# Flamingo block on one core: the last mixture of experts sorted once for all tokens, its tiles run in six steps, with another order of stages

## The chip, the cores and the metric

The kernel runs on one core of a Trainium2 chip. The metric is the device time of one execution in microseconds (us); lower is better. A core has five engines that run at the same time: TensorE (PE; its weight loads are shown as PEld), VectorE (DVE), ScalarE (ACT), GpSimd (POOL) and SyncE (SP), which here only issues DMAs. Each engine takes its instructions strictly in order: an instruction that waits holds all that stand behind it. Sixteen DMA engines move data for all queues. POOL issues the DMAs whose row numbers come from a table (indirect ones); SP issues nearly all others.

## The reference

The input `x` has 16 batches of 256 tokens of 128 values, all float32: 4096 tokens. Four layers follow; each adds a cross attention to a context of 64 keys (16 heads of 8) and then a feed-forward part, both after a layernorm and both times a tanh gate:

```python
x = x + tanh(g_xattn[0]) * L0_xattn(layernorm(x), ctx, ctx, ...)   # softmax over heads
x = x + tanh(g_ffn[0])   * L0_ffn(layernorm(x), ...)               # 8 experts, top 2, and a shared one
x = x + tanh(g_xattn[1]) * L1_xattn(...)                           # with a bias on the scores
x = x + tanh(g_ffn[1])   * L1_ffn(...)                             # ternary weights, 128x128
x = x + tanh(g_xattn[2]) * L2_xattn(...)
x = x + tanh(g_ffn[2])   * L2_ffn(...)                             # comes down to one expert
x = x + tanh(g_xattn[3]) * L3_xattn(...)
x = x + tanh(g_ffn[3])   * L3_ffn(...)                             # 8 experts, top 1: the last mixture
```

The last mixture, which the change is about:

```python
logits = t @ switch_w + switch_b                 # t: 4096 x 128
route_prob = softmax(logits)
route_prob_max, routes = max(route_prob), argmax(route_prob)
for e in range(8):
    h = gelu(t @ w1[e] + b1[e])                  # 128 -> 512
    y = h @ w2[e] + b2[e]                        # 512 -> 128
    out = where(routes == e, y, out)
out = out * route_prob_max
```

## The kernel before

**Halves, stages, blocks.** The 16 batches are cut into two halves of 8. Each half goes through eight stages: 0 and 1 are the first layer's attention and mixture, 2 and 3 the second's attention and ternary product, 4 and 5 the third's attention and expert, 6 and 7 the fourth's attention and mixture. Attention works on a batch, layernorm and feed-forward on a block of two batches (512 tokens, four tiles of 128). `X[i][b]` is the event that batch b has come to stage i. Both halves are under way at once.

**A planner writes the order.** Every piece of work is a generator (a task with a rank) that asks for the next instruction, with an estimated length and the events and buffers that it needs. `Order.run` takes the request that can begin first by these estimates (rounded to 0.1 us), and of several the one with the lowest rank. The result is a fixed order on PE, DVE, ACT, SP and POOL. The plan's times are not waited for on the chip: a DMA task that is planned "when X[5][b] has come" only has its place in SP's order from that. Real waits come from the framework, which follows who writes and reads each tile or tensor. `RANKS` gives each half's eight stages their rank.

**A mixture by sorted tiles.** Tokens are sorted by expert, so that a tile of 128 rows has one expert. For each tile the kernel loads one expert's packed weights (592 KB, `fetch`, L1822, six buffers `wb`), gets the tile's rows, transposes them (L1867), multiplies by W1 (L1881), applies gelu (L1888), multiplies by W2 (L1902), and on DVE adds the bias (L1912) and, in the last mixture, the gate and the old x (L1919). The first mixture gathers rows by an index (L1853, POOL), stores sorted results and collects them (`collect`, L1971 and L1979).

**The last mixture** (`last_mixture`) is run once for each half. A half has a tensor `xrow3{hf}` in HBM with a region of 2048 rows for each of 8 experts, and 128 rows between; a row holds the normed token, the old x, the token's number and its gate (1032 bytes). Each block normalizes, does the gate matmul (L1618), softmax and largest entry, counts how many of its tokens go to each expert (L1653), puts the running counts in `next_`, and POOL scatters its four tiles of rows to their places (L1681). When all four blocks of the half are counted, one table is made on DVE (L1702 to L1739): which expert each tile has, and from which row it starts. Each expert's last tile may be partly empty, so a half has 16 + 7 = 23 tiles, 46 in all. SP fetches a tile's 128 rows at a row number read from the table (L1848). Results are scattered by POOL straight to the output (L1947), empty rows to a number out of bounds.

**Filling.** Since a tile may read rows that no token was put in, `fill_regions` writes defined values into the tensors ahead of time: 27 DMAs of 645 KB for each half (L1804), placed in SP's order by the events X[5] and X[6] of the first half for the first tensor, and X[3] and X[4] of the second half for the second. Other loads on SP at that time are the score bias of the second attention (L312, through three buffers).

Of the kernel before, what the change touches and what calls it, by code (L numbers as in the profile page):

```python
# [75 lines left out]
REGION = NT * P  # L76
NROWS = E * REGION + (E - 1) * P


def sorted_tiles(k):  # L80

    return k * NT + E - 1
# [10 lines left out]
RANKS = ((10, 14, 14, 1, 1, 12, 8, 14), (14, 14, 2, 7, 5, 9, 10, 15))  # L93
# [116 lines left out]
def op(engine, length, *needs, table=None):  # L210
    return ("op", engine, length, needs, table)
# [6 lines left out]
def get(slots, number, *needs):  # L218
    return ("get", slots, number, needs, None)
# [24 lines left out]
def flamingo_kernel(  # L244
# [37 lines left out]
    def slots(name, shape, n, dtype=F32):  # L282
        return Slots([cst(shape, f"{name}_{i}", dtype) for i in range(n)])
# [52 lines left out]
    for l, k in ((0, 2), (3, 1)):  # L336
        n = sorted_tiles(k)
        for hf in range(2):
            size = [NT * P, D] if l == 0 else [NROWS, ROW3]
            xd = dram.tile(size, F32, name=f"xrow{l}{hf}", tag=f"xrow{l}{hf}")  # L340
            yd = None
            if l == 0:
                yd = dram.tile([n * P, D], F32, name=f"ysort{l}{hf}", tag=f"ysort{l}{hf}")
            srt[l, hf] = (k, n, xd, yd)
# [101 lines left out]
    state_s = slots("state", [P, 4 * NT + nmax], 2)  # L446
# [3 lines left out]
    expert_s = slots("expert", [1, 2 * (nmax + 7)], 2, I32)  # L450
# [1126 lines left out]
    def last_mixture(hf, rank, begin):  # L1577
# [6 lines left out]
        _, n, xd, _ = srt[l, hf]  # L1584
        b0 = HB * hf
        blks = range(NBLK // 2 * hf, NBLK // 2 * (hf + 1))
        (st,) = yield get(state_s, 1, begin[b0], moe_ready)
        (ex,) = yield get(expert_s, 1)
        pos = st.ap[:, 0:NT].bitcast(I32)

        next_ = st.ap[:, 4 * NT : 4 * NT + E]
        yield op(DVE, 0.1, st)
        nc.vector.tensor_copy(next_, region)
        kept = Event(len(blks) * 4)
        counted = Event(len(blks))
# [7 lines left out]
        def block(blk):  # L1603
            t0 = 4 * (blk - blks[0])
# [65 lines left out]
            order.set(counted, at)  # L1670
# [7 lines left out]
            for t in range(t0, t0 + 4):  # L1678
                at = yield op(POOL, 1.3, placed)
                part_indirect()  # L1680
                ins = nc.gpsimd.indirect_dma_start(  # L1681
                    out=xd,
                    out_offset=bass.IndirectOffsetOnAxis(ap=pos[:, t : t + 1], axis=0),
                    in_=rows[:, t - t0, :],
                    in_offset=None,
                )
                unordered(ins, f"x{l}{hf}")
                at = (at[0] + 2.2, "DMA")
                order.set(kept, at)
            give(xn, big_s, at)  # L1690

        for blk in blks:
            order.task(rank, block(blk))

        (sc,) = yield get(xf_s, 1, counted)
# [3 lines left out]
        yield op(DVE, 0.6, counted, sc)  # L1701
        nc.vector.tensor_tensor(cn, next_, region, ALU.subtract)  # L1702
        nc.vector.tensor_scalar(cn.bitcast(I32), cn, float(P - 1), None, ALU.add)
        nc.vector.tensor_scalar(cn.bitcast(I32), cn.bitcast(I32), -P, None, ALU.bitwise_and)
        nc.vector.tensor_copy(pad, cn.bitcast(I32))
        nc.vector.tensor_tensor_scan(ends, ones[:, 0:E], pad, 0.0, ALU.mult, ALU.add)
        nc.vector.tensor_scalar(skip, pad, -1.0, float(REGION), ALU.mult, ALU.add)
# [19 lines left out]
        known = yield op(DVE, 0.0026 * n * (E - 1) * 2 + 0.15)  # L1727
        by_tile(skip[:, 0 : E - 1], sums)
        nc.vector.tensor_tensor(rowf, sums, starts[:, 0:n], ALU.add)
        nc.vector.tensor_copy(ex_r, rowf[0:1])  # L1730

        filled, empty = (st.ap[:, NT + n * i : NT + n * (i + 1)].bitcast(I32) for i in range(2))
        at = yield op(DVE, 1.1)
        nc.vector.tensor_tensor(skip[:, 0 : E - 1], next_[:, 1:], next_[:, 0 : E - 1], ALU.subtract)
        by_tile(skip[:, 0 : E - 1], sums)
        nc.vector.tensor_scalar(sums, sums, next_[:, 0:1], None, ALU.add)
        nc.vector.scalar_tensor_tensor(rowf, rowf, place_of, sums, ALU.add, ALU.is_lt)
        nc.vector.tensor_scalar(filled, rowf, -1.0, None, ALU.mult)
        nc.vector.tensor_scalar(empty, rowf, -2.0 * B * S, 2.0 * B * S, ALU.mult, ALU.add)  # L1739
# [3 lines left out]
        ex.users, st.users = 2 * n, n  # L1743
        order.task(rank, fetch(l, hf, ex, known, room, fetched))
        for q in range((n + 1) // 2):
            order.task(
                rank + 0.001 * q,
                sorted_pair(
                    l, hf, q, st, ex, (at, kept), room[q], fetched[q], None, filled, empty
                ),  # L1750
            )
# [33 lines left out]
    def unordered(ins, group):  # L1785

        tc.declare_no_dep(ins.ins, group=group, reason="rows are unique")
        tc.add_to_no_dep_group(group, ins.ins)
        scatters.add(ins.ins.name)
# [9 lines left out]
    def fill_regions(hf, whens):  # L1799
        xd = srt[3, hf][2].rearrange("(p a) c -> p a c", p=P)  # L1800
        n, m = NROWS // P, 5
        for i in range(n // m):
            yield dma(SP, 4.0 * P * m * ROW3, whens[i * m * len(whens) // n])
            nc.sync.dma_start(  # L1804
                xd[:, m * i : m * (i + 1), :],
                rows_sb[:, 0:ROW3].unsqueeze(1).to_broadcast([P, m, ROW3]),
            )

# [18 lines left out]
    def sorted_pair(l, hf, q, st, ex, needs, room, fetched, stored, filled=None, empty=None):  # L1827
# [82 lines left out]
        for i in range(m):  # L1910
            yt = yield op(DVE, 0.25 if l == 0 else 0.75, at, y)
            nc.vector.tensor_tensor(  # L1912
                yi[i], py.ap[:, i * D : (i + 1) * D], wb[i].ap[:, PK_B2 : PK_B2 + D],
                ALU.add,
            )
            give(wb[i], wb_s, yt)
            if l == 3:
                t = 2 * q + i
                nc.vector.scalar_tensor_tensor(  # L1919
                    yi[i], yi[i], xg[i][:, 2 * D + 1 :], xg[i][:, D : 2 * D], ALU.mult, ALU.add  # L1920
                )

                nc.vector.tensor_tensor(
                    place[:, i : i + 1], xg[i][:, 2 * D : 2 * D + 1].bitcast(I32),
                    filled[:, t : t + 1], ALU.bitwise_and,
                )
                nc.vector.tensor_tensor(  # L1927
                    place[:, i : i + 1], place[:, i : i + 1], empty[:, t : t + 1], ALU.bitwise_or
                )
                give(xgs[i], xg_s, yt)  # L1930
# [58 lines left out]
    def rank(stage, hf, i=0):  # L1989
        return RANKS[hf][stage] + 0.01 * i  # L1990
# [5 lines left out]
    for hf in range(2):  # L1996
# [26 lines left out]
        order.task(rank(7, hf), last_mixture(hf, rank(7, hf), X[7]))  # L2023

    whens = [X[i][b] for i, h in ((5, 0), (6, 0), (3, 1), (4, 1)) for b in range(HB * h, HB * h + HB)]
    for hf in range(2):
        order.task(100.0, fill_regions(hf, whens[16 * hf : 16 * hf + 16]))
# [92 lines left out]
```

## Time and profile before

Nine runs: median 1078.47 us, 1071.66 to 1086.42. The profiled execution took 1091.43 us, of which the span from the first instruction to the last is 1089.7.

| | busy us | share of the span | in 700 to 900 us |
|---|---|---|---|
| PE | 916.1 | 84% | 191 of 200 |
| PEld | 729.0 | 67% | 134 of 200 |
| DVE | 690.7 | 63% | 150 of 200 |
| POOL | 633.3 | 58% | 114 of 200 |
| ACT | 586.3 | 54% | 130 of 200 |

DMA queues moved 150 MB. Marks on the time line, from the starts of instructions: the first mixture's tiles run from 188 to 317 (first half) and 363 to 530 (second half); the second attention from 388 to 720; the third and fourth from 550 to 950; gate matmuls of the last mixture's eight blocks begin at 812, 857, 875, 897, 918, 939, 953 and 977; its tiles run from 934 to 1080.

A line of instructions in the profile gives the kernel's line, engine, operation, tiles (output, arrow, inputs), count, then busy us and mean ns, then idle time before it and what ended it. "busy" says nothing of whether an instruction's work was on the path to the end; the chain of waits follows that path back from the last instruction.

### The profile page before, as it was taken

How to read it: one execution, taken by the hardware profiler on the slowest of the kernel's cores; microseconds unless marked ns; L12 is line 12 of the kernel's file. 1: busy time of each engine (PE TensorE's matmuls, PEld its weight loads, DVE VectorE, ACT ScalarE, POOL GpSimd, SP SyncE). 2: the span in 40 equal slices, each digit the busy share in tenths (PEclk: the TensorE clock that was granted, in tenths of full speed). 3: DMA queues.
4: the chain of work that ended last, by engine and by line, in shares of the span. 5: the costliest groups of instructions: out<-in, count | busy, mean ns of one | idle time of the engine just before them, and what ended most of it. 6: DMA issues, size and time to landing. Idle time of an engine off the chain costs nothing.

```text
span 1089.7 us, 28097 instructions
## 1 busy us (share of the span) xinstructions
PE 916.1 (84%) x10472; PEld 729.0 (67%) x10472; DVE 690.7 (63%) x2027; ACT 586.3 (54%) x1369; POOL 633.3 (58%) x1032
## 2 busy tenths in 40 slices
PE   5888577979879797889888799999999997977875
PEld 3776345868776686767756577766666664767775
DVE  4797897754348244545667578977766787555333
ACT  6454343675544354666647447675775664654432
POOL 5786636668646746663357554353456786465443
PEclk9898779989989988899989889999999998998988
DMA  6000104366852555564562931999900005277782
GB/s 195 2 12 12 32 1 145 114 229 227 271 144 66 182 165 179 186 215 132 132 123 59 210 77 43 225 223 224 208 6 21 12 26 186 95 248 240 257 291 96
DMA packets 96280, 150.14 MB, mean 138 GB/s; under 512 B 11281, under 2 KB 75800, under 8 KB 96144
## 3 DMA queue, kind: packets, MB, share of 16 engines
q1 hardware_dynamic: 88160, 131.77, 43.6%
q0 software_dynamic: 7552, 15.65, 5.0%
q8 instruction: 82, 1.34, 0.5%
q10 hardware_dynamic: 432, 0.93, 0.3%
q14 instruction: 54, 0.44, 0.1%
HBM read 99.11 MB, written 50.12 MB: 137 GB/s over the span
## 4 chain that ended last, share of the span: by engine, by line
PE 35%; DVE 17%; DMA 6%; POOL 5%; issue 5%; ACT 2%; SPq 1%; POOLq 0%; another core or an unknown queue 0%; DVEq 0%; ACTq 0%
PE bank L1881 6%; PE bank L1902 5%; PE bank L1033 4%; PE bank L1200 3%; DVE mx L1118 3%; DMA xg<-xrow,state 3%; PE bank L1159 2%; PE bank L1097 2%; DMA yg<-ysort,state 2%; PE bank L1039 2%; DVE mx L1071 1%; PE bank L806 1%; PE bank L1222 1%; DVE ln L669 1%; DVE pT L1079 1%
## 5 line engine op out<-in xcount | busy, mean ns | idle before, releaser
L1888 ACT ACTIVATE big<-bank,wb 128x128 f32<-128x128 f32 x496 | 138.7, 380 | 120.3 <-issue 66.2
L1881 PE MATMUL bank<-xgT,wb 128*128 128x128 f32 x992 | 145.2, 300 | 29.4 <-DVE y L1927 15.3
L1881 PEld LDWEIGHTS bank<-xgT,wb 128*128 128x128 f32 x992 | 132.0, 210 | 40.2 <-DVE y L1927 16.9
L1902 PE MATMUL bank<-wb,big 128*128 128x128 f32 x992 | 135.0, 290 | 2.2 <-ACT big L1888 2.0
L1902 PEld LDWEIGHTS bank<-wb,big 128*128 128x128 f32 x992 | 127.9, 205 | 4.9 <-ACT big L1888 2.9
L681 ACT ACTIVATE xn<-x,ln 128x128 f32<-128x128 f32 x224 | 94.1, 493 | 50.9 <-POOL ln L675 50.5
L1971 POOL DMA_INDIRECT yg<-ysort,state x64 | 63.7, 995 | 65.4 <-DMA ysort<-y 29.2
L919 POOL TENSOR_TENSOR pT<-pT,rc 128x1024 f32<-128x1024 f32 x32 | 75.1, 2363 | 37.8 <-DVE rc L902 9.5
L1118 DVE TENSOR_REDUCE mx<-bank 128x8 f32<-128x512 f32 x128 | 81.1, 681 | 15.8 <-PE bank L1039 7.9
L1912 DVE TENSOR_TENSOR y<-bank,wb 128x128 f32<-128x128 f32 x124 | 32.3, 286 | 92.2 <-PE bank L1902 72.8
L1853 POOL DMA_INDIRECT xg<-xrow,state x78 | 76.7, 983 | 13.7 <-issue 7.6
L1033 PE MATMUL bank<-kexp,qT 32*128 32x256 f32 x768 | 74.0, 427 | 11.2 <-DVE pT L1079 10.9
L1947 POOL DMA_INDIRECT out_dram<-y x46 | 46.6, 1012 | 62.8 <-DVE y L1912 57.1
L702 POOL TENSOR_TENSOR x<-x,rows_sb 128x256 f32<-128x256 f32 x96 | 71.8, 764 | 15.5 <-ACT xn L681 14.7
L672 POOL TENSOR_SCALAR ln<-ln 128x4 f32<-128x4 f32 x64 | 14.8, 232 | 110.7 <-DVE ln L670 101.5
L1187 ACT ACTIVATE pT<-bank 128x512 f32<-128x512 f32 x128 | 67.2, 601 | 21.5 <-PE bank L1174 20.6
L1871 DVE COPY xgT<-bank 128x256 f32<-128x256 f32 x64 | 26.3, 413 | 69.4 <-PE bank L1867 52.8
L669 DVE BATCH_NORM_STATS2 ln<-x 128x6 f32<-128x128 f32 x256 | 68.5, 267 | 2.6 <-DMA x<-in_x_dram 2.3
L673 POOL TENSOR_TENSOR ln<-ln,mhalf 128x4 f32<-128x4 f32 x64 | 66.9, 1045 | 5.3
L1103 ACT ACTIVATE pT<-bank 128x512 f32<-128x512 f32 x64 | 37.6, 599 | 39.2 <-PE bank L1097 36.8
L1200 PE MATMUL bank<-pT,vx 128*32 128x256 f32 x768 | 58.3, 401 | 0.2 <-ACT pT L1103 0.2
L1033 PEld LDWEIGHTS bank<-kexp,qT 32*128 32x128 f32 x768 | 37.5, 193 | 23.6 <-DVE pT L1079 12.1
(269 smaller groups left out, 2187.3 us busy)
## 6 DMA issues: line engine op xcount, KB each, us to landing
wb<-in_pk_l_dram SPq DMA_DIRECT2D x124, 578.0 KB
xrow<-rows_sb SPq DMA_DIRECT2D x54, 645.0 KB
xg<-xrow SPq DMA_DIRECT2D x46, 129.0 KB
ysort<-y SPq DMA_DIRECT2D x38, 128.0 KB
fill<-in_fsideT_dram SPq DMA_DIRECT2D x64, 64.0 KB
x<-in_x_dram SPq DMA_DIRECT2D x16, 128.0 KB
xrow<-xn SPq DMA_DIRECT2D x8, 256.0 KB
xg<-xrow,state POOLq DMA_INDIRECT x78
```

The lines of the kernel that those rows point to most:

```text
L669: nc.vector.bn_stats(st[:, 2 * i + j, :], xs[b][:, j, :])
L681: nc.scalar.activation(xn[:, k, :], xs[b][:, j, :], AF.Identity, bias=nm[:, k : k + 1], scale=rs[:, k : k + 1],)
L702: nc.gpsimd.tensor_tensor(xs[b], xs[b], row.unsqueeze(1).to_broadcast([P, 2, D]), ALU.add)
L919: nc.gpsimd.tensor_tensor(s3, s3, rc.ap.unsqueeze(1).to_broadcast([P, 8, P]), ALU.mult)
L1033: nc.tensor.matmul(dst(g), qT[strip(g), ts], kexp[strip(g)].rearrange("p h k -> p (h k)"), start=True, stop=False,)
L1118: nc.vector.tensor_reduce(mx[:, :, g, :], sc[g].ap.rearrange("p (t h k) -> p t h k", h=4, k=S2), AX.X, ALU.max,)
L1187: nc.scalar.activation(pTs[g // 2].ap[:, (g % 2) * 512 : (g % 2 + 1) * 512], sc[g].ap, AF.Exp)
L1200: nc.tensor.matmul(po.ap[strip(g), i * S : (i + 1) * S], vx.ap[:, b % 2, c, :], pTs[c // 4].ap[:, (c % 4) * S : (c % 4 + 1) * S], start=Tr ...
L1853: nc.gpsimd.indirect_dma_start(out=xg[i], out_offset=None, in_=xd, in_offset=bass.IndirectOffsetOnAxis(ap=index[:, 2 * q + i : 2 * q + i + ...
L1881: nc.tensor.matmul(ph.ap[:, cs], wb[i].ap[:, cs], xgT.ap[:, i * P : (i + 1) * P], start=True, stop=True,)
L1888: nc.scalar.activation(two(hb)[:, i, cs], ph.ap[:, cs], func, bias=wb[i].ap[:, PK_B1 + c : PK_B1 + c + 1],)
L1902: nc.tensor.matmul(py.ap[:, i * D : (i + 1) * D], two(hb)[:, i, c * P : (c + 1) * P], wb[i].ap[:, PK_W2 + c * D : PK_W2 + (c + 1) * D], st ...
```

## The change

The last mixture is no longer run for each half. There is one tensor of rows for all 4096 tokens, with regions of 4096 rows, and one running count. Blocks of both halves are put into it as they come. After 3, 4, 5, 6, 7 and 8 blocks a step begins, with 5, 4, 4, 4, 4 and 18 tiles: 39 in all, 32 + 7. So many full tiles there must be after that many blocks, however the tokens fall; tiles of a step but the last are full, so their output needs no marking of empty rows. `held` keeps how much of each region earlier steps have taken. Each step makes a table of its own, and its order is `told` by the step before. A scatter of rows needs, in the plan, that all filling is done; the filling has 53 DMAs of 645 KB, all placed by X[5] of the first half. Ranks of several stages change. The steps' tiles have the rank of stage 7 of the first half (for the first two) or the second.

```diff
-REGION = NT * P
-NROWS = E * REGION + (E - 1) * P
+REGION = B * S
+NROWS = E * REGION + (E + 1) * P
+STEPS = ((3, 5), (4, 4), (5, 4), (6, 4), (7, 4), (8, 18))
...
-RANKS = ((10, 14, 14, 1, 1, 12, 8, 14), (14, 14, 2, 7, 5, 9, 10, 15))
+RANKS = ((8, 14, 14, 11, 1, 11, 11, 16), (14, 14, 2, 14, 5, 12, 13, 15))
+FILL = (5,)
...
-        for hf in range(2):
-            size = [NT * P, D] if l == 0 else [NROWS, ROW3]
-            xd = dram.tile(size, F32, name=f"xrow{l}{hf}", tag=f"xrow{l}{hf}")
...
+    regions = dram.tile([NROWS, ROW3], F32, name="xrow3", tag="xrow3")
+    for i, (_, n) in enumerate(STEPS):
+        srt[3, i] = (1, n, regions, None)
...
-            order.set(counted, at)
+            blocks_counted[0] += 1
+            mine_of = [i for i, (k, _) in enumerate(STEPS) if blocks_counted[0] <= k]
+            for i in mine_of:
+                if blocks_counted[0] == STEPS[i][0]:
+                    nc.vector.tensor_copy(snap[i], upto3[:, :, 4])
+                    order.set(counted[i], at)
...
-                at = yield op(POOL, 1.3, placed)
+                at = yield op(POOL, 1.3, placed, regions_filled)
...
-                unordered(ins, f"x{l}{hf}")
+                unordered(ins, "x3")
                 at = (at[0] + 2.2, "DMA")
-                order.set(kept, at)
+                for i in mine_of:
+                    order.set(kept[i], at)
...
+        for blk in range(NBLK):
+            rank = rank_of(7, blk // (NBLK // 2))
+            order.task(rank, block(blk, rank))
+        ex_at = [sum(n for _, n in STEPS[:i]) for i in range(len(STEPS) + 1)]
+        for i, (k, n) in enumerate(STEPS):
+            order.task(
+                rank_of(7, int(k > NBLK // 2)) + 0.0005 * i,
+                step(
+                    i, n, st, snap[i], held, Slot(ex.ap[:, 2 * ex_at[i] : 2 * ex_at[i + 1]]),
+                    counted[i], kept[i], tables, rank_of(7, int(k > NBLK // 2)) + 0.1 * i,
+                ),
+            )
...
+    def step(i, n, st, seen, held, ex, counted, kept, tables, rank):
+        l, last = 3, i == len(STEPS) - 1
+        (sc,) = yield get(xf_s, 1, counted, tables[i])
...
+        nc.vector.tensor_tensor(cn, seen, region, ALU.subtract)
+        nc.vector.tensor_scalar(cn.bitcast(I32), cn, float(P - 1 if last else 0), None, ALU.add)
...
+        nc.vector.tensor_scalar(skip, pad, -1.0, float(REGION), ALU.mult, ALU.add)
+        nc.vector.tensor_tensor(pad, pad, held, ALU.subtract)
         nc.vector.tensor_tensor_scan(ends, ones[:, 0:E], pad, 0.0, ALU.mult, ALU.add)
+        nc.vector.tensor_tensor(
+            skip[:, 0 : E - 1], skip[:, 0 : E - 1], held[:, 1:], ALU.add
+        )
...
+        else:
+            at = yield op(DVE, 0.3)
+            nc.vector.tensor_tensor(ends, pad, ends, ALU.subtract)
+            nc.vector.tensor_scalar(ends, ends, float(P * n), 0.0, ALU.add, ALU.max)
+            nc.vector.tensor_tensor(ends, ends, pad, ALU.min)
+            nc.vector.tensor_tensor(held, held, ends, ALU.add)
+        order.set(tables[i + 1], at)
...
-    def fill_regions(hf, whens):
-        xd = srt[3, hf][2].rearrange("(p a) c -> p a c", p=P)
+    def fill_regions(whens):
+        xd = regions.rearrange("(p a) c -> p a c", p=P)
         n, m = NROWS // P, 5
         for i in range(n // m):
-            yield dma(SP, 4.0 * P * m * ROW3, whens[i * m * len(whens) // n])
+            at = yield dma(SP, 4.0 * P * m * ROW3, whens[i * m * len(whens) // n])
...
+        order.set(regions_filled, at)
...
+                token = xg[i][:, 2 * D : 2 * D + 1].bitcast(I32)
+                if filled is None:
+                    nc.vector.tensor_copy(place[:, i : i + 1], token)
...
-        order.task(rank(7, hf), last_mixture(hf, rank(7, hf), X[7]))
-    whens = [X[i][b] for i, h in ((5, 0), (6, 0), (3, 1), (4, 1)) for b in range(HB * h, HB * h + HB)]
-    for hf in range(2):
-        order.task(100.0, fill_regions(hf, whens[16 * hf : 16 * hf + 16]))
+    order.task(rank(7, 0) - 0.001, last_mixture(X[7]))
+    order.task(100.0, fill_regions([X[i][b] for i in FILL for b in range(HB)]))
```

## The prediction

> **What bounds the kernel now.** I read the page first, then busy time by stretch, then the SyncE timeline of the last 190 us, then the chain of waits and the wait table.
>
> ```profile
> span 1089.7 us, 28097 instructions
> PE 916.1 (84%) x10472; PEld 729.0 (67%) x10472; DVE 690.7 (63%) x2027; ACT 586.3 (54%) x1369; POOL 633.3 (58%) x1032
> PE   5888577979879797889888799999999997977875
> DMA  6000104366852555564562931999900005277782
> L1881 PE MATMUL bank<-xgT,wb 128*128 128x128 f32 x992 | 145.2, 300 | 29.4 <-DVE y L1927 15.3
> L1902 PE MATMUL bank<-wb,big 128*128 128x128 f32 x992 | 135.0, 290 | 2.2 <-ACT big L1888 2.0
> ```
>
> TensorE is busy for 84% of the span and over 90% in slices 27 to 33 (about 710 to 900 us). Before and after that it has holes, and the last 190 us are another regime: that is where the last mixture's tiles run. One tile is eight L1881 and eight L1902 matmul records, so 124 tiles (78 of the first mixture, 46 of the last) cost (145.2 + 135.0) / 124 = 2.26 us of TensorE each.
>
> Busy time in 20 us stretches (columns: length, then busy time of PE, PEld, DVE, ACT, POOL with counts, granted clock, DMA share, GB/s):
>
> ```profile
> 900.00:920.00 20.00, 14.93 (x179) 10.53 (x182) 15.07 (x57) 8.51 (x19) 11.23 (x20) 0.83 0.58 209
> 920.00:940.00 20.00, 16.23 (x194) 11.32 (x191) 10.47 (x47) 11.15 (x26) 10.21 (x19) 0.83 0.21 64
> 940.00:960.00 20.00, 19.20 (x194) 17.15 (x195) 13.80 (x62) 16.75 (x41) 11.65 (x23) 1.00 0.57 184
> 960.00:980.00 20.00, 13.86 (x105) 13.39 (x103) 9.91 (x50) 8.97 (x31) 12.65 (x21) 0.91 0.77 246
> 1040.00:1060.00 20.00, 15.49 (x111) 15.02 (x110) 6.11 (x27) 6.76 (x25) 8.58 (x14) 0.85 0.87 288
> ```
>
> From 900 to 940 TensorE stands idle for 5.07 + 3.77 = 8.8 us while the first half's 23 tiles are not yet to be had; from 1000 on the DMA engines are 0.8 to 0.9 busy and TensorE about 0.77: the tail is held by weights and rows arriving together with matmuls at a reduced clock.
>
> SyncE's queue in that time (weights at L1822, a tile's rows at L1848):
>
> ```profile
> 907.43 7.14 SPq L1822 DMA_DIRECT2D wb<-in_pk_l_dram  x6
> 918.21 6.12 SPq L1848 DMA_DIRECT2D xg<-xrow  x6
> ...
> 1009.86 2.46 SPq L1848 DMA_DIRECT2D xg<-xrow  x2
> ...
> 1069.95 0.33 SPq L1848 DMA_DIRECT2D xg<-xrow  x1
> ```
>
> The first half's tiles run from 918 to 1003, the second half's 23 from 1009.86 to 1069.95: 22 intervals in 60.1 us, **2.73 us a tile**, and the kernel ends a fixed 20 us after the last fetch. The last attention unit ends at 958 (the last L812), the last gate matmul is at 978, the last table at 1000: 50 us from the last attention to the first tile of the second half, in which the first half's leftovers run.
>
> **The change, part by part.** All sums are against the profiled execution's 1091.43 us (span 1089.7 and 1.7 around it), 1.2% above the median 1078.47; differences are carried to the median unscaled (1.2% of 20 us is nothing).
>
> (a) *The last run of tiles is 18, not 23.* Five fewer at 2.73 us: **-13.7 us**. It counts in full if the last block's chain still sets when the last step starts; bounds 5 x 2.26 = 11.3 (TensorE alone) and 5 x 2.93 = 14.7 (matmuls from 1013 to 1080.4, over 23).
>
> (b) *21 tiles instead of 23 ahead of it.* Two at 2.26 us: **-4.5**; 0 if they only leave holes.
>
> (c) *Tiles can start after three blocks.* Gate matmuls are at 813, 857, 875 and 897 for the first half; the first tile's matmul comes at 934, because the table (904 to 909) and the last scatters (to 911.6) wait for the fourth block. Five tiles are now free after the third. Three of them fit the 8.8 us hole (6.8 us): **-6.8**, bounds 0 and -8.8.
>
> (d) *Six tables for two.* The first half's table took 904.3 to 909.3, 5.0 us on VectorE for 18 instructions; a step's has 19 and the last some six more. Four more are 20 us of VectorE, which in 900 to 980 is busy for 49 of 80 us: 31 us cover it. If the cover were gone it is 20 us. What is queued behind a table is the y and xgT work of tiles: **+1**, bounds 0 and 20.
>
> (e) *One tensor of rows for scatters and fetches.* Before, no fetch of a half came ahead of a scatter of that half. Now blocks 4 to 8 (20 scatters on POOL) are written between fetches on SP from the same tensor. That fetches wait for scatters of the tensor is in the trace; that scatters wait for fetches is not, but the framework orders by tensor and only scatters among themselves are exempted, so I expect it.
>
> ```profile
> SPq L1848 <- DMA xrow<-big,state: 2.8, 1, 2.8
> ```
>
> The chain of waits has the time of a fetch, and (550 and 594) of gathers that meet the fills:
>
> ```profile
> 550.76 8.72 DMA yg<-ysort,state
> ...
> 594.52 8.27 DMA yg<-ysort,state
> ...
> 1009.86 3.10 DMA xg<-xrow
> 1018.45 5.13 DMA xg<-xrow
> ```
>
> A scatter that waits for a fetch holds POOL for 3.1 to 5.1 us, and behind it the next block's layernorm, which ACT and TensorE then wait for; a fetch that waits for a scatter holds SP for 2.8 or more, and behind it weight loads. Five bursts of (2.8 + 3.1 to 5.1) make 30 to 40 us of queue time. POOL is idle for 34 us in 900 to 980, and six weight buffers stand ahead of SP, so most is covered: **+3**, bounds 0 and 40.
>
> The Trainium skill (DMA: Bandwidth & Descriptors, "Anatomy of one DMA") speaks against this part: a DMA costs about 2.0 us plus its bytes at 436 GB/s, and the receipt takes longest where the target is HBM. By it a fetch of 129 KB is 2.3 us, less than the 3.10 to 5.13 shown, and five bursts would be some 22 us, also covered; the measured rows decide.
>
> (f) *Fills.* 53 of 645 KB for 54, so the same bytes, but all are due in the plan when the first half's third attention ends. SP ran ahead of that in the trace:
>
> ```profile
> L1804 SPq DMA_DIRECT2D xrow<-rows_sb x54: 420/2704/4290, 531.9 to 780.9; - x54
> ```
>
> 18 came by 655, among the second half's score-bias loads (L312) and gathers (L1971); the other 36, after the last of those loads, took 680.6 to 780.9, 2.87 us each, with TensorE over 95% busy: they cost nothing. 53 are 152 us of the DMA engines, now mostly between those loads. In the two bursts shown gathers took 8.7 and 8.3 us, about 3 over the 5.4 of xg gathers without fills (459.89). Six more such bursts would be 18 us; three bias buffers and the other half's attention cover most. **+4**, bounds -6 (the two vanish) and 30. First scatters wait for the last fill, but gates begin at 813: slack of over 50 us.
>
> The skill's rule in the same page ("Queues, rings and completion order") is that each DMA engine goes round the queues by packet. By that a POOL gather beside SP's fills gets half the rate and no more, and the term would be about 0; the 8.72 us says it is worse.
>
> (g) *Stage order.* The ternary stage falls behind the second half's attention, both last attentions fall a little. From 660 to 900 TensorE is full in any order; from 540 to 640 it is idle for 16.0 us, which a better order could fill or a worse one double: **0**, bounds -16 and +16.
>
> Sum: -13.7 - 4.5 - 6.8 + 1 + 3 + 4 = -17.0, so 1078.5 - 17.0 = **1061 us**, on the profile 1074.
>
> **Rivals.**
> - *Fetches and scatters hold each other up (slower).* If the plan alternates them in every block twice, ten alternations at 2.8 + 5.1 us are 79 us; less the 34 us of idle POOL, 45 remain on the way to the last block's gate. 1061 - 3 + 45 = 1103; with half of the alternations waiting on the path, 1083. It decides from about 20 us on the path, that is some seven alternations. For it: both queues are in order and the plan has no such cost. Against it: fetches are issued in pairs as buffers come free, so many fall together. Chance 0.17, 1083 to 1103.
> - *Fills in the wrong place (slower).* A burst per batch is 53 / 8 x 2.87 = 19 us of the wire; if in two bursts out of three the second half's bias load or gather comes 5 us later than TensorE's in-order queue can bear, 27 us: 1061 - 4 + 27 = 1084. For it: 550.76 and 594.52. Against: prefetch. Chance 0.15.
> - *No change.* The work moved ahead of the last block (nine more tiles before it than the 12 done by 978) delays its gate by 9 x 2.26 = 20 us and gives the 17 back: 1078, give or take 5. Against it: 8.8 us are holes and the last 11 leftovers ran in the 50 us behind the last attention. Chance 0.11.
> - *Far more.* TensorE idles for about 43 us between 900 and 1083; if tiles and order fill half of it besides (a) and (b), 1078.5 - 18.2 - 21 = 1039, and with -10 of (g) 1029. Chance 0.13.
>
> **How the numbers follow.** The forecast (1045 to 1072) has 0.44. Differences below 0.5% (5.4 us) can't be told from none here. Faster: 0.44 + 0.13 = 0.57; slower: 0.17 + 0.15 = 0.32; same 0.11. The range 1033 to 1097 leaves out the ends of the first and the last rival; the forecast's own is 1045 to 1072.
>
> **What would show it.** (a, b) 312 L1881 matmuls for the last mixture instead of 368, last fetch to end still 20 us, last run 18 tiles at about 2.7 us. (c) First tile's matmul soon after the third gate, the hole gone. (d) Six tables, none in the chain. (e) Waits of L1681 on xg fetches, and L1848 on scatters, in the wait table; over 20 us of POOL's before the last gate means the first rival. (f) TensorE below 80% busy in 540 to 700 with waits for L312 or yg means the second. I am wrong if the last attention ends more than 15 us after 958: then the time was lost ahead of the stage that was changed.

## The result, and the profile after

The changed kernel is slower: median 1101.6 us (20 runs) beside 1081.92 for the kernel before on the same chip (62 runs), ratio 1.018 with the interval 1.0157 to 1.0203. The forecast was 1061 and the range ended at 1097. The profiled execution has a span of 1110.9 us against 1089.7; both profiled executions took 1% longer than the median of their kernel.

The page of the kernel after: span; busy time by engine; PE and DMA in 40 slices; then rows of instructions, of which the first is the W1 product of the tiles (L1936, formerly L1881) and the second the addition of collected rows of the first mixture (L2038, formerly L1979).

```profile
span 1110.9 us, 27720 instructions
PE 915.9 (82%) x10353; PEld 724.1 (65%) x10353; DVE 690.1 (62%) x2057; ACT 578.2 (52%) x1341; POOL 622.1 (56%) x1015
PE   5887569898878878889885898899999986788783
DMA  6001004547834564645999999500000032266681
L1936 PE MATMUL bank<-xgT,wb 128*128 128x128 f32 x936 | 141.2, 305 | 21.1 <-DVE xgT L1926 11.5
L2038 DVE SCALAR_TENSOR_TENSOR x<-yg,state,x 128x128 f32<-128x128 f32 x64 | 21.6, 362 | 58.1 <-DMA yg<-ysort,state 54.8
```

936 products are 117 tiles, 78 + 39: the seven tiles are gone, and TensorE's busy time did not fall (915.9 for 916.1): its mean granted clock was 0.905 where it had been 0.921, and 1.7% of 916 us is about as much as seven tiles of 2.26 us. The two rows of slices say where the DMA engines went: the run of nines stands in slices 20 to 25 (528 to 694 us), under which PE has 8, 8, 5, 8, 9, 8. Before, it stood in slices 26 to 29.

Starts of instructions (for the ternary product, of the last group of eight) mark the stages. "Ahead" is the number of tiles of the last mixture whose results were scattered before the last attention was added to x:

| | last ternary product | last attention | end of span | tiles ahead |
|---|---|---|---|---|
| before | 743 | 958 | 1089.7 | 4 of 46 |
| after | 771 | 1002 | 1110.9 | 9 of 39 |

The stretch behind the last attention became 23 us shorter (131.7 to 108.9). But 28 us were lost ahead of the last ternary product, and 16 more between that and the last attention. The time was lost ahead of the stage that was changed, which is what I had written as the sign that I was wrong.

**The first loss, 540 to 700 us.** Busy time in that stretch (length; PE, PEld, DVE, ACT, POOL with counts; granted clock; DMA share; GB/s), of the kernel before:

```profile
540.00:700.00 160.00, 143.10 (x1654) 101.83 (x1649) 118.22 (x332) 91.36 (x194) 93.52 (x178) 0.94 0.55 119
```

and after:

```profile
540.00:700.00 160.00, 129.41 (x1503) 93.26 (x1502) 101.36 (x289) 80.79 (x175) 84.84 (x162) 0.91 1.04 221
```

The DMA share went from 0.55 to 1.04, TensorE lost 13.7 us of work in 160. The fills (the row of L1858, formerly L1804: duration of the issue, first and last start) now run from 529 to 695; before, 36 of 54 came after 680:

```profile
L1858 SPq DMA_DIRECT2D xrow<-rows_sb x53: 372/2136/4157, 529.4 to 694.8; - x53
```

The chain of waits after (start, length, what) has two kinds of work that meet them:

```profile
502.26 5.65 DMA xg<-xrow,state
...
548.21 7.47 DMA yg<-ysort,state
...
556.40 7.83 DMA yg<-ysort,state
...
569.28 8.41 DMA yg<-ysort,state
...
578.45 9.57 DMA yg<-ysort,state
...
601.24 8.91 DMA yg<-ysort,state
...
671.57 15.49 DMA xrow<-rows_sb
687.07 11.23 DMA xrow<-rows_sb
698.30 0.43 PE bank L1040
```

Five gathers of sorted results (yg) on the path took 7.5 to 9.6 us; the one at 502, of rows (xg) and before the fills, 5.65. From 671.57 to 698.30 the path is the fills themselves: between 666 and 693.9 no score product (L1040) starts, and the one at 698.30 waits again; TensorE has other work for 19.9 of these 27 us. SyncE's queue says why (start, length, line, count): the score-bias loads L320 are behind 13 fills in the same in-order queue.

```profile
654.72 13.11 SPq L320 DMA_DIRECT2D fill<-in_fsideT_dram  x8
667.88 11.31 SPq L1858 DMA_DIRECT2D xrow<-rows_sb  x7
679.30 4.56 SPq L320 DMA_DIRECT2D fill<-in_fsideT_dram  x4
683.91 14.14 SPq L1858 DMA_DIRECT2D xrow<-rows_sb  x6
698.16 4.18 SPq L320 DMA_DIRECT2D fill<-in_fsideT_dram  x3
```

The wait table (engine, line, what it waited for: total us, times, longest) before, and then after:

```profile
DVE x L1979 <- DMA yg<-ysort,state: 31.5, 11, 7.0
```

```profile
DVE x L2038 <- DMA yg<-ysort,state: 54.8, 13, 8.5
...
POOL xrow L1698 <- DMA xg<-xrow: 5.5, 1, 5.5
```

**The second loss, scatters and fetches.** The last line of that table is new: a scatter of rows that waits for a fetch. SyncE's own waits after have the other direction, a fetch that waits for a scatter, in the second line here (before: one wait of 2.8); the first is the wait for a step's table:

```profile
SPq L1873 <- DVE xf L1750: 25.1, 3, 22.6
SPq L1903 <- DMA xrow<-big,state: 19.4, 3, 7.7
```

and the chain after shows both, one behind the other:

```profile
962.52 5.01 DMA xg<-xrow
...
968.31 2.90 DMA xrow<-big,state
...
971.33 2.19 DMA xg<-xrow
...
1034.89 6.36 DMA xrow<-big,state
...
1042.98 1.73 DMA xg<-xrow
```

A fetch of 5.01 us holds a scatter, the scatter's landing the next fetch. That makes two suspects, the places of the fills and the shared tensor; the new ranks are a third. The experiments undo each alone.

### The profile page after: what moved, and what is told of

It is laid out like the page before. It is cut to its first block, busy times and chain, and to the rows that moved or that the text cites. A ratio compares the mean times of both kernels' runs of the same rounds, so it can differ in the third digit from the quotient of the medians.

```text
span 1110.9 us, 27720 instructions
## 1 busy us (share of the span) xinstructions
PE 915.9 (82%) x10353; PEld 724.1 (65%) x10353; DVE 690.1 (62%) x2057; ACT 578.2 (52%) x1341; POOL 622.1 (56%) x1015
## 4 chain that ended last, share of the span: by engine, by line
PE 29%; DVE 17%; DMA 12%; POOL 5%; issue 5%; ACT 2%; SPq 1%; another core or an unknown queue 0%; DVEq 0%; POOLq 0%; ACTq 0%
PE bank L1936 5%; DVE mx L1125 4%; DMA yg<-ysort,state 4%; PE bank L1957 3%; DMA xg<-xrow,state 3%; PE bank L1040 3%; DMA xrow<-rows_sb 2%; PE bank L1207 2%; PE bank L1104 2%; PE bank L1166 1%; PE bank L1046 1%; DMA xg<-xrow 1%; DVE ln L676 1%; POOL xrow L1698 1%; PE bank L813 1%
## 5 line engine op out<-in xcount | busy, mean ns | idle before, releaser
L1943 ACT ACTIVATE big<-bank,wb 128x128 f32<-128x128 f32 x468 | 130.4, 378 | 116.3 <-issue 56.1
L1936 PE MATMUL bank<-xgT,wb 128*128 128x128 f32 x936 | 141.2, 305 | 21.1 <-DVE xgT L1926 11.5
L1936 PEld LDWEIGHTS bank<-xgT,wb 128*128 128x128 f32 x936 | 128.1, 215 | 33.1 <-DVE xgT L1926 16.3
L1957 PE MATMUL bank<-wb,big 128*128 128x128 f32 x936 | 123.1, 284 | 3.2 <-ACT big L1943 2.4
L1957 PEld LDWEIGHTS bank<-wb,big 128*128 128x128 f32 x936 | 116.5, 199 | 6.1 <-ACT big L1943 3.1
L1908 POOL DMA_INDIRECT xg<-xrow,state x78 | 76.5, 980 | 13.7 <-issue 9.1
L1194 ACT ACTIVATE pT<-bank 128x512 f32<-128x512 f32 x128 | 67.5, 603 | 29.3 <-PE bank L1181 23.7
L1040 PE MATMUL bank<-kexp,qT 32*128 32x256 f32 x768 | 72.3, 422 | 5.8 <-DVE mx L1125 3.0
L2006 POOL DMA_INDIRECT out_dram<-y x39 | 39.5, 1013 | 52.8 <-DVE y L1967 42.4
L1926 DVE COPY xgT<-bank 128x256 f32<-128x256 f32 (+1 forms) x60 | 24.8, 414 | 64.5 <-PE bank L1922 50.7
L2038 DVE SCALAR_TENSOR_TENSOR x<-yg,state,x 128x128 f32<-128x128 f32 x64 | 21.6, 362 | 58.1 <-DMA yg<-ysort,state 54.8
L1698 POOL DMA_INDIRECT xrow<-big,state x32 | 32.9, 1027 | 42.1 <-DVE xgT L1926 8.8
```

What stands on the lines that cost most here:

```text
L1040: nc.tensor.matmul(dst(g), qT[strip(g), ts], kexp[strip(g)].rearrange("p h k -> p (h k)"), start=True, stop=False,)
L1194: nc.scalar.activation(pTs[g // 2].ap[:, (g % 2) * 512 : (g % 2 + 1) * 512], sc[g].ap, AF.Exp)
L1908: nc.gpsimd.indirect_dma_start(out=xg[i], out_offset=None, in_=xd, in_offset=bass.IndirectOffsetOnAxis(ap=index[:, 2 * q + i : 2 * q + i + ...
L1936: nc.tensor.matmul(ph.ap[:, cs], wb[i].ap[:, cs], xgT.ap[:, i * P : (i + 1) * P], start=True, stop=True,)
L1943: nc.scalar.activation(two(hb)[:, i, cs], ph.ap[:, cs], func, bias=wb[i].ap[:, PK_B1 + c : PK_B1 + c + 1],)
L1957: nc.tensor.matmul(py.ap[:, i * D : (i + 1) * D], two(hb)[:, i, c * P : (c + 1) * P], wb[i].ap[:, PK_W2 + c * D : PK_W2 + (c + 1) * D], st ...
```

## The experiments

Ratios are against runs of the kernel before on the same chip. The chips differ (its median was 1044 to 1084 us), so kernels of different groups are compared by ratio, with the intervals' half widths added as squares; 0.001 is about 1.05 us.

**The fills at their old places.** The changed kernel with the 53 fills spread by the events of before:

```diff
-    order.task(100.0, fill_regions([X[i][b] for i in FILL for b in range(HB)]))
+    order.task(100.0, fill_regions([X[i][b] for i, h in ((5, 0), (6, 0), (3, 1), (4, 1))
+                                    for b in range(HB * h, HB * h + HB)]))
```

> The changed kernel with one thing undone: its 53 fills are placed by the 32 events of before (X[5] and X[6] of the first half, X[3] and X[4] of the second) and not by X[5] of the first half alone. Theory F (the fills, put among the second half's bias loads and gathers, cost the middle): the last third-layer ternary comes 20 us or more earlier than 771, PE over 86% busy in 500 to 700, and the time falls by 20 to 28 us, to about 1078, ratio near 1.00. Theory W (scatters and fetches of one tensor wait for each other in the last 150 us): the time falls by less than 8 us. Theory O (the new ranks starve the second half): by less than 8 us.

Measured: 1057.11 us, 1.0078 (1.0043 to 1.0113). The row of the fills and the stretch 540 to 700 of this kernel:

```profile
L1858 SPq DMA_DIRECT2D xrow<-rows_sb x53: 372/2629/3810, 508.8 to 747.1; - x53
```

```profile
540.00:700.00 160.00, 145.39 (x1802) 105.56 (x1801) 125.11 (x355) 98.99 (x213) 89.64 (x174) 0.98 0.61 138
```

TensorE has its 16 us back in that stretch, the whole kernel 1.0% (0.6 to 1.4), less than the 20 to 28 us expected. So the places of the fills cost about 11 us, and 0.8% remain that are something else.

**The old order of stages.** The changed kernel with the `RANKS` of before:

```diff
-RANKS = ((8, 14, 14, 11, 1, 11, 11, 16), (14, 14, 2, 14, 5, 12, 13, 15))
+RANKS = ((10, 14, 14, 1, 1, 12, 8, 14), (14, 14, 2, 7, 5, 9, 10, 15))
```

> The changed kernel with the ranks of before. Theory O: the time falls by 15 us or more, to below 1087, and the last attention unit ends within 15 us of 958 instead of at 1002. Theories F and W: fills and tensor stay, so no more than 8 us of change either way.

Measured: 1090.01 us, 1.039 (1.0331 to 1.0449): worse by 2.1% than with the new ranks. The new order belongs to the new places of the fills: it softens them.

**Scatters that don't wait for earlier fetches.** The rows that an earlier step fetches are never those that a later block writes, so the order between them can be given up (such waits are called false in what follows):

```diff
                 unordered(ins, "x3")
+                for read in fetches:
+                    tc.declare_no_dep(ins.ins, read, reason="other rows")
...
-                nc.sync.dma_start(xg[i], xd[bass.ds(r, P), :])
+                ins = nc.sync.dma_start(xg[i], xd[bass.ds(r, P), :])
+                fetches.append(ins.ins)
```

> The changed kernel, in which scatters no longer wait for fetches that were issued before them (they touch other rows: a fetch of a step reads full tiles of blocks counted earlier). Fetches still wait for earlier scatters. Theory W: GpSimd's waits on xg fetches (5.5 us at 968 and others) vanish and the last attention ends earlier; 10 to 25 us less, 1077 to 1091. Theories F and O: under 5 us.

Measured: 1064.41 us, 1.0116 (1.0058 to 1.0175), 0.6% less than after with an uncertainty as large. By itself this settles little; the same edit where the fills are not in the way is e6 and e7.

**The fills' new places alone, in the kernel before.**

```diff
...
-        order.task(100.0, fill_regions(hf, whens[16 * hf : 16 * hf + 16]))
+        order.task(100.0, fill_regions(hf, [X[5][b] for b in range(4 * hf, 4 * hf + 4)]))
```

> The kernel before with one part of the change: its 54 fills are placed by X[5] of the first half (27 by batches 0 to 3, 27 by 4 to 7). Theory F: PE falls from about 90% to 83% in 500 to 700 and the time rises by 12 to 25 us, ratio 1.011 to 1.023. Theories W and O: ratio within 0.995 to 1.005.

Measured: 1089.65 us, 1.0357 (1.0281 to 1.0433): this alone makes the kernel before 3.6% slower. Its stretch 540 to 700:

```profile
540.00:700.00 160.00, 129.60 (x1496) 94.75 (x1492) 105.23 (x295) 78.76 (x167) 80.77 (x159) 0.89 0.91 201
```

129.6 us of TensorE, as in the changed kernel (129.41), with no step, no merged tensor and no new rank in it. The 64 gathers that collect sorted results (last number: median us from issue to landing) are slower too; here this kernel, and then e5 below, which has the fills at their old places:

```profile
yg<-ysort,state POOLq DMA_INDIRECT x64, 8.8
```

```profile
yg<-ysort,state POOLq DMA_INDIRECT x64, 2.7
```

**Only the steps.** The changed kernel with the fills' places and the ranks of before (the edits of e1 and e2):

> Steps and one sort alone: the changed kernel with both the fills' places and the ranks of before. If the parts simply add (e2 1.039 less e4 1.036), the ratio is 1.000 to 1.006: the seven tiles saved are worth nothing net, because scatters and fetches wait for each other. If the predicted gain of the steps (some 24 us) is there and only the fills hid it, 0.975 to 0.985.

Measured: 1056.77 us, 1.0109 (1.0052 to 1.0165). Seven tiles fewer, nothing lost at 540 to 700, and still 1.1% slower. SyncE's waits in it:

```profile
SPq L1903 <- DMA xrow<-big,state: 30.5, 6, 5.7
```

**The steps, with scatters free of earlier fetches** (e5 with the edit of e3):

> As e5, and scatters no longer wait for earlier fetches (other rows). If these waits eat the gain of the steps: 8 to 20 us below e5, ratio 0.98 to 0.995. If they are covered: within 4 us of e5.

Measured: 1041.98 us, 0.9964 (0.9925 to 1.0004). The false waits cost 1.45% (0.75 to 2.15), some 15 us, and without them the steps are about where the kernel before is. Waits of fetches for scatters, which this edit leaves in place, are half of what they were:

```profile
SPq L1908 <- DMA xrow<-big,state: 15.6, 5, 5.5
```

**New ranks, old fills, free scatters** (after with the edits of e1 and e3):

> The new ranks with the old places of the fills (e1), and scatters that don't wait for earlier fetches (e3). If the two costs add (1.018 to 1.0078, and 1.018 to 1.0116): ratio 1.000 to 1.003. If they are the same loss seen twice: about 1.007.

Measured: 1044.24 us, 0.9984 (0.9952 to 1.0015). So the 1.8% of the changed kernel can be split in three steps: steps and ranks together -0.2% (before to e7), the false waits +0.9% (e7 to e1), the fills +1.0% (e1 to after). The shares depend on the order of undoing: with the fills in the way, freeing the scatters is worth 0.6% (e3).

**The new ranks alone, in the kernel before:**

> The kernel before with the new ranks alone. If the new order is itself slow (ternary of the second half behind all of the first): ratio 1.005 to 1.015, which would be all of what is left in e1. If it is neutral: 0.997 to 1.003, and what is left in e1 belongs to the steps.

Measured: 1063.34 us, 1.018 (1.0128 to 1.0233). The new order costs the kernel before 19 us; in the steps it costs nothing to be seen (e6 to e7: +0.2%, uncertain by 0.5). No tile of the last mixture ran ahead of the last attention in it.

**Is the plan's ignorance what spoils the steps?** The plan takes a scatter to land 2.2 us after its start, and lets no fetch wait for the newest scatter. Here e6 with both told to it:

```diff
-                at = (at[0] + 2.2, "DMA")
+                at = (at[0] + 6.5, "DMA")
+                newest[0] = at
...
-                yield op(SP, 0.4, *xgs, *needs)
+                yield op(SP, 0.4, *xgs, *needs, newest[0])
```

> e6 (steps, old places of the fills, old ranks, scatters free of earlier fetches), and the plan is told what the chip showed: a scatter's rows count as landed 6.5 us after the scatter (2.2 before), and a fetch comes behind the newest scatter's landing. If what is left of the steps' gain is lost because SP stands before fetches that wait for scatters of later blocks (15.6 us in e6's wait table), the new order avoids some of it: 4 to 12 us below e6, ratio 0.985 to 0.993. If it is lost in the chain from the last attention to the last step (TensorE busy 8.9 of 20 us in 960 to 980 of e6), no order helps: within 4 us of e6.

Measured: 1086.01 us, 1.0016 (0.9982 to 1.0049). No gain. But the waits that the new plan was to avoid are not fewer, 28.5 us where e6 has 15.6:

```profile
SPq L1910 <- DMA xrow<-big,state: 28.5, 3, 20.4
```

So this run shows that this plan does not help, and not what those waits cost.

**Fewer steps.** e6 with two, and the plan of e9 with three and the blocks ranked ahead of the tiles:

```diff
-STEPS = ((3, 5), (4, 4), (5, 4), (6, 4), (7, 4), (8, 18))
+STEPS = ((6, 17), (8, 22))
```

```diff
-STEPS = ((3, 5), (4, 4), (5, 4), (6, 4), (7, 4), (8, 18))
+STEPS = ((5, 13), (7, 8), (8, 18))
...
-            order.task(rank, block(blk, rank))
+            order.task(13.5, block(blk, rank))
```

> e6 with two steps, 17 tiles after six blocks and 22 after all eight, for six. Theory cover (early tiles only leave the chain behind the last attention without work to cover it; the end is that chain and the last run): tiles are left for the hole, but the last run has 22 tiles, four more at 2.7 us; ratio 0.995 to 1.01, TensorE over 14 of 20 us busy in the 20 us ahead of the last run. Theory alternation (the number of times that scatters and fetches change places is what costs): 5 us or more below e6.

> As e9 with three steps, 13 tiles after five blocks, 8 after seven, 18 after eight, and the blocks' own work at rank 13.5, ahead of tiles. Theory cover: between e9 and e10, 0.99 to 1.00, with the last step earlier after the last attention since its block is not behind tiles. Theory alternation: below e9.

Measured: 1077.29 us, 0.9969 (0.9929 to 1.0008), and 1081.28 us, 0.997 (0.993 to 1.001). In both, no tile ran ahead of the last attention; in e6 11 did, in e7 four. All four lie between 0.996 and 0.999, each uncertain by 0.3 to 0.4%. **Among these four, the number of tiles that run ahead of the last attention makes no difference that can be seen**: what is gained behind it is paid ahead of it. In the profiles the last attention is at 90.2% of the span in e6 and 89.5% in e7, but at 87.5 and 87.3% in e10 and e11 (before: 87.9). No version is shown to be faster than the kernel before.

**What is a tile worth?** My forecast had 18 us for seven tiles fewer, and e6 has 4. So tiles were taken out of both kernels: seven of the late ones, or 21 of the early ones.

```diff
-            srt[l, hf] = (k, n, xd, yd)
+            srt[l, hf] = (k, 16 if (l, hf) == (3, 1) else n, xd, yd)
```

```diff
-            srt[l, hf] = (k, n, xd, yd)
+            srt[l, hf] = (k, 2 if (l, hf) == (3, 0) else n, xd, yd)
```

> The kernel before with 16 tiles instead of 23 in the second half of the last mixture; the last 7 tiles' work is left out. If a tile of the last run costs the 2.73 us that I charged, it is 7 x 2.73 = 19 us shorter, ratio about 0.982; if the tail is bound by the wait for its rows and weights and not by the number of tiles, it is under 8 us shorter, above 0.993.

> The kernel before with 2 tiles instead of 23 in the first half of the last mixture; 21 tiles' work is left out. If they cost TensorE's time and no more, 21 x 2.26 = 47 us, ratio about 0.956. If much of them runs in time that is idle anyway (the 50 us between the last attention and the second half's first tile, of which they fill a part), less than 25 us, above 0.977.

In the steps the table itself is shortened, to a last entry of (8, 11), or to (8, 18) alone:

```diff
-STEPS = ((3, 5), (4, 4), (5, 4), (6, 4), (7, 4), (8, 18))
+STEPS = ((3, 5), (4, 4), (5, 4), (6, 4), (7, 4), (8, 11))
```

```diff
-STEPS = ((3, 5), (4, 4), (5, 4), (6, 4), (7, 4), (8, 18))
+STEPS = ((8, 18),)
```

> The kernel of e6 with 11 tiles instead of 18 in its last step; 7 tiles' work is left out. Same two prices as k1, against e6's 0.9964: about 0.978 if a last tile costs 2.73 us, above 0.989 if it costs under 1.1 us. If k1 shows 19 us and this shows much less, the last run of the steps is bound by something else than its tiles, and the term for five fewer of them fell there.

> The kernel of e6 with the last step alone: 18 tiles after all eight blocks, no earlier ones; 21 tiles' work and five tables are left out. If the early tiles cost the same in steps as in halves, the distance from e6 is that of k2 from the kernel before. If their late rows stand in TensorE's queue ahead of the last attentions, it is over 10 us more than in k2.

| | ratio (interval) | what the tiles left out were worth | last ternary to last attention | tiles ahead |
|---|---|---|---|---|
| k1, before less 7 late | 0.9934 (0.9888 to 0.998) | 7 us (2 to 12) | 203 us | 4 |
| k2, before less 21 early | 0.9861 (0.9793 to 0.9929) | 15 us (7 to 22) | 199 us | 2 |
| e6 | 0.9964 (0.9925 to 1.0004) | | 231 us | 11 |
| k3, steps less 7 late | 0.9761 (0.9689 to 0.9833) | 21 us (13 to 30) | 233 us | 11 |
| k4, steps less 21 early | 0.9641 (0.9556 to 0.9726) | 34 us (24 to 44) | 199 us | 0 |

(The third column is the distance of the ratio from 1, or from e6's, times 1050 us. k4 leaves out five tables too.) In the kernel before, a late tile is worth 1.0 us (0.3 to 1.7) and an early one 0.7 (0.3 to 1.0); in the steps 3.0 (1.8 to 4.2) and 1.6 (1.1 to 2.1). In the kernel before most of the early tiles fill the time between the last attention and the second half's first tile, which has to pass anyway. With 21 of them gone (k2), this is what is left there:

```profile
940.00:960.00 20.00, 1.85 (x7) 1.26 (x8) 5.88 (x28) 1.28 (x1) 4.92 (x8) 0.50 0.68 238
```

In the steps 11 tiles go ahead of the last attention, and the way to it from the last ternary product is 32 us longer than without them (231 to 199; 11 x 2.26 = 25 us of TensorE are in it, the rest was not taken apart). The whole order is planned anew in k4: its last ternary product comes later, so that on the clock of the two profiles the last attention differs by 19 us (937.9 to 919.2, on two chips). And then these tiles are missing as cover for the last block. e6's stretch 960 to 980, and TensorE in it (start, length, line, what, count, in brackets idle time before and what ended it):

```profile
960.00:980.00 20.00, 8.86 (x39) 7.65 (x39) 9.10 (x48) 3.45 (x9) 9.06 (x16) 0.61 0.56 178
```

```profile
937.06 0.38 PE L1928 MATMUL bank<-ident,xg 128*128 128x128 f32 x2
939.79 0.33 PE L1928 MATMUL bank<-ident,xg 128*128 128x128 f32 x1 [2.34 <-DMA xg<-xrow]
941.18 0.48 PE L1928 MATMUL bank<-ident,xg 128*128 128x128 f32 x1 [1.07 <-DMA xg<-xrow]
941.66 5.49 PE L1942 MATMUL bank<-xgT,wb 128*128 128x128 f32 x24
946.94 0.84 PE L701 MATMUL bank<-ident,big 128*128 128x128 f32 x4
948.45 1.06 PE L1630 MATMUL bank<-gw,xf 128*128 128x8 f32 x8 [0.67 <-ACT xf L703]
...
956.01 1.95 PE L1963 MATMUL bank<-wb,big 128*128 128x128 f32 x16
...
968.71 3.79 PE L1942 MATMUL bank<-xgT,wb 128*128 128x128 f32 x16 [6.69 <-DVE xgT L1932]
972.57 3.06 PE L1963 MATMUL bank<-wb,big 128*128 128x128 f32 x16
978.06 0.44 PE L1928 MATMUL bank<-ident,xg 128*128 128x128 f32 x1 [2.42 <-DMA xg<-xrow]
```

Two things are to be seen. The transposes of the last block (L701) stand behind a tile whose rows come late: TensorE waits 2.34 and 1.07 us for the rows, then does 24 products, and the block's normed rows (the activation ended at 943.74) are taken at 946.94. And from 962.02 TensorE has nothing more to do: the copy that the next products need (L1932) is behind the last block's counting and the last table on VectorE, 6.69 us. Then comes the chain of that kernel, a scatter and a fetch:

```profile
968.78 7.13 DMA xrow<-big,state
...
977.03 2.10 DMA xg<-xrow
```

## Why the prediction was wrong

Three steps failed: the price of a tile ((a) to (c), -25 us in the sum, -4 in e6), the false waits of the shared tensor ((e), +3, measured 10 to 15) and the places of the fills ((f), +4, measured 11). By the prediction's own steps, in its order:

- **(a) Five fewer last tiles, -13.7, bounds -11.3 to -14.7: with (b) and (c) the largest error.** k1 has 7 us (2 to 12) for seven, so five are worth 5 (1.5 to 8.4) in the kernel before. I read 2.73 us from the distance of neighbouring fetches in the tail. That is how fast tiles go, not what the end of the kernel gains when some are gone. The lower bound by TensorE's busy time (2.26) was no bound: the engine is busy for 63 of the 80 us from 1000 to 1080. Why a late tile in the kernel before is worth only 1.0 us was not found; k1's order is planned anew and is not the old one less seven tiles. In the steps a late tile is worth 3.0 us (k3), about the price that I charged. So the price belongs to the order that the tile is in, and how the 21 us that are missing divide among (a), (b) and (c) stays open; that they are missing is what e6 shows.
- **(b) Two fewer early ones, -4.5; (c) an earlier start, -6.8.** An early tile of the kernel before is worth 0.7 us (k2), so (b) is 1.4. I had named it: "0 if they only leave holes". For (c) I set three tiles into an 8.8 us hole at 900 to 940. In the changed kernel the third gate matmul is at 886 and the first fetch at 911.7 (before 918.2), but the first tile's product comes at 936.2 (before 934.0), and TensorE is busy for 31.6 us in 900 to 940 where it was for 31.2: the hole is still there. In e6 the tiles start 62 us ahead of the last attention, 11 of them come before it, and the way to it is 32 us longer than in k4, so nothing was left. The forecast's sum for (a), (b) and (c) was -25 us; e6, without the two added costs but still with fetches that wait for scatters, shows -4 (-8 to 0). This is the rival that I called "No change": nine tiles ahead of the last gate that cost TensorE what they save later. Its mechanism fits e6, and I gave it 0.11 because "8.8 us are holes".
- **(d) Six tables, +1.** Not told apart by a run of its own. The last table did what I had set down as its price without cover: copies for tiles stand behind it, 6.69 us of idle TensorE in e6; and after, SyncE waits once for 22.6 us for a table.
- **(e) One tensor, +3, bounds 0 to 40.** Waits both ways, as predicted, and the size wrong. Freeing scatters from fetches alone is worth 15 us (8 to 23) with old ranks (e5 to e6), 10 (5 to 15) with new ones (e1 to e7). I covered it with 34 us of idle POOL and six weight buffers. As I read the chain, idle time of the engine that waits is no cover where the instructions behind the wait make the next block's rows and the next fetch. (The 2.3 us that the prediction takes from the Trainium skill stand in a section on DMAs that GpSimd issues; the fetches are SyncE's.) In the first rival, half of its 45 us would make 1080.5, not 1083.
- **(f) Fills, +4, bounds -6 to 30.** 11 us (6 to 15) with the new ranks, 30 (21 to 38) with the old (e2 to e5), 38 (30 to 46) in the kernel before (e4). This is the second rival, which I priced at 27 us and gave 0.15. I had its sign in hand, 550.76 and 594.52 with gathers of 8 us beside 18 fills, and put 53 into the same stretch, covered by "three bias buffers". Three buffers don't help when seven fills stand between two groups of loads in the same queue (667.88). The 5.4 us that I set beside them as a gather without fills was the shortest of three on that chain (5.42, 7.42, 6.08), and of another kind; medians of the same gather are 2.7 and 8.8 (e5, e4). The mark that I had set, TensorE under 80% in 540 to 700, was just missed (129.41 of 160 is 81%), but before it was 89%.
- **(g) Stage order, 0, bounds -16 to +16.** +19 (13 to 24) alone in the kernel before (e8), about at the bound; with the steps and old fills +2; with the steps and misplaced fills -22 (e2 to after). It has no price of its own, only one beside the fills' places.

Each rival had its chance as if one of them came true. Three did at once: fills +11, false waits +10, and tiles that gain nothing, in place of a gain of 25. None of them excludes another, and the chances left no room for two at once.

What stays open: fetches still wait for the newest scatter of the tensor, though it is of a later block (15.6 us in five waits in e6). Taking that away as well wasn't tried. That it would bring the missing gain is not shown. Why a late tile is worth 1.0 us in one order and 3.0 in the other is open too.

## What to carry to other kernels

The price of a piece of work is what the end gains when it is taken out, and this is often much less than its busy time or its interval: work that covers a fixed chain is cheap (0.7 us for an early tile of 2.26), and moving it ahead of that chain takes away the cover and delays the chain. A bulk transfer with much slack belongs where the queue it is issued from has no load that someone waits for; moving two thirds of the same bytes from 680 to 780 us into 510 to 700 cost the kernel before 38 us (30 to 46). When two tensors become one, list every pair of writer and reader that is now ordered, on which in-order queue each of them waits, and what stands behind it.

## What the runs showed of the hardware

- A scatter of 128 rows of 1032 bytes by POOL, at the places where the path went through it: 2.55 to 2.90 us from its start to its landing in the five cases in which the DMA share was 0.32 or less meanwhile (2.90 at 968.31 of the changed kernel, share 0.14; the others in e1 and e2), and 4.00 to 7.13 us in the twelve with a share of 0.51 or more (6.36 at 1034.89 of the changed kernel, 0.51; 7.13 in e6, 0.99). The Trainium skill (DMA: Bandwidth & Descriptors, "Anatomy of one DMA") says that the fixed 2.0 us of a DMA are mostly the receipt of the last byte, and longest where the target is HBM. By its figures 132 KB would be an estimated 2.3 us: near the scatters at a low share, and a third of the longest. Which part of a scatter grows with the load is not shown here.
- A hole costs more than its length. In e6, 16 products took 1.95 us at 956.01; after 6.69 us of idle TensorE 16 of the same shape took 3.79 at 968.71. The granted clock was 1.00 from 950 to 956 and 0.50 from 962 to 972.5. The Trainium skill (TensorE: Matmul & The Clock Gate, "What's actually happening") has the rule: an array that was idle for some 3.4 us runs at half the clock until it has been busy for as long. The factor of 1.94 agrees. My sums took idle time as lost by its length alone.
